# First stage of a graph kernel: products of a constant ahead of the first weights, second weights turned around the second tile's product, counts from the first tile on

## The chip, the cores and the metric

The kernel runs on one core of one Trainium2 chip. The metric is the device time of one execution in microseconds (us), as the median of several runs; lower is better. A core has TensorE (PE in the profile; its weight loads are PEld), VectorE (DVE), ScalarE (ACT), GpSimd (POOL), SyncE (SP) and 16 DMA engines. A small q behind an engine's name (SPq, POOLq) means its sequencer, which issues DMAs.

## The reference, cut to what matters

The network has four graph layers over 2708 nodes with 512 features; the adjacency matrix is 2708 x 2708, int32, zeros and ones. The change touches the first layer only:

```python
def _L0_gnn_ref(X, A, W_nb, b_nb, W_line, b_line, neibor_num):      # neibor_num = 64
    Ab = A > 0
    keep = Ab & (jnp.cumsum(Ab.astype(jnp.int32), axis=1) <= neibor_num)
    cnt = keep.sum(axis=1, keepdims=True).astype(X.dtype)
    nb_sum = keep.astype(X.dtype) @ X
    nb_mean = nb_sum / jnp.maximum(cnt, 1.0)
    xj = jax.nn.leaky_relu(nb_mean @ W_nb.T + b_nb)
    xi = jax.nn.leaky_relu(X @ W_line.T + b_line)
    return xi + jnp.where(cnt > 0, xj, jnp.zeros((), X.dtype))

x = _layernorm(x + _L0_gnn_ref(x, adj, ..., 64), axis=-1)
# then layers 1 to 3: a mean over neighbours, and two attention layers with 8 heads
```

## The kernel before, in words

Nodes are cut into 22 tiles of 128 rows (the last has 20); `rows(t)` is the height of tile t. The first stage, of some 200 us, computes three things for every tile t: `product(xT, n, wnT, ...)`, which is X times W_nb, kept as a high and a low part (`keep_y`: the high part `yH` by ACT at L241, the low part `yL` by DVE at L246); X times W_line plus its bias (`u`, added by DVE at L417, stored to `r0_dram` from POOL's queue at L418); and the masks of `HERE` = 14 of the 22 row blocks of the adjacency matrix, turned around into the resident `maskT`. The other eight masks are made in the stage behind it, while PE already multiplies masks with the kept parts.

**Weights.** `transpose_weight` (L139) fetches a 512 x 512 weight in four pieces of 128 rows into `room` (parts of `maskT` not yet in use), turns each piece with four PE transposes into a tile `ps_tr` (L146) and copies that with DVE (L147). `ps_tr` has two buffers, which the transposes of the x tiles (L134, copied by ACT at L136) use too. W_nb is turned ahead of tiles 0 and 1, W_line behind them.

**Order.** PE's order in this stage is written out by hand: `pe(ins)` (L105) ties each PE instruction behind the one before. The other queues are ordered by the framework's scheduler, which takes an instruction when by its own estimate it is ready, earlier program lines first; `tc.issue_after(ins)` holds the instructions of a block behind `ins` on its engine. The order of an engine's queue is fixed when the program is built; on the chip an engine waits for the instruction that is next in it.

**Masks.** A mask block `m` (128 x 2708 int32, cast to bf16 by the load at L282 on POOL's queue) has three buffers. Its unused last columns are cleared first: by DVE for the first two blocks, behind `weights_made`, the last copy of the turned W_line (L354); by POOL for later ones (L356). Block by block, `count` (L287, ACT, 128 x 2708) makes zeros and ones and sums them; `place` (L289) runs twice, each time on one half of the columns: a running sum (L293, DVE scan) and a product (L296, DVE). The first half is held behind the tile's `yL`, the second behind the tile's `u`. Then `turn_next` turns the block: even ones by a DMA from SP's queue (L314), with ACT taking the signs two tiles later (L319); odd ones, and those from 12 on, by 22 PE transposes (L305), with signs by ACT (L309).

**Loop.** In the main loop over t (L388) PE's order in one tile is: product with W_nb (for t > 1; tiles 0 and 1 have theirs already), the transposes of x tile t + 1, transposes of a mask if one is due, product with W_line. The sums of the W_line products lie in `pm1`, a PSUM tile with one buffer: the next such product waits until DVE has added the bias (L417). Sums of W_nb products alternate between `pm0` and a tile from `sums()`. A line decides in which tiles a block is counted:

```python
now = counted < min(HERE, -(-(t - 1) * HERE // (NT - 5)))
```

With HERE = 14 and NT = 22 this counts in tiles 2 to 6, 8 to 12 and 14 to 17; tiles 0, 1, 7 and 13 count nothing.

Of the kernel before, what the change touches and what calls it, by code (L numbers as in the profile page):

```python
# [19 lines left out]
P = 128  # L20
D = 512
KD = D // P
# [9 lines left out]
def kernel(  # L32
# [9 lines left out]
    nc = tc.nc  # L42
    N = x.shape[0]
    NT = -(-N // P)
# [6 lines left out]
    def rows(t):  # L51
        return min(P, N - t * P)
# [9 lines left out]
    ident = const.tile([P, P], F32, name="ident")  # L62
# [4 lines left out]
    ones = const.tile([P, P], F32, name="ones")  # L67
# [37 lines left out]
    def pe(ins):  # L105

        for i in ins.ins if isinstance(ins.ins, tuple) else (ins.ins,):
            if behind:
                tc.add_manual_dep(i, behind[0], mybir.DependencyInfo(
                    mybir.DependencyClass.NoSync, mybir.DependencyReason.DATA), reason="order")  # L110
            behind[:] = [i.name]
# [27 lines left out]
    def transpose_weight(room, psum, dst, src, queues=(nc.sync,)):  # L139

        for ki in range(KD):
            wr = room[ki]
            queues[ki % len(queues)].dma_start(wr, src[ki * P:(ki + 1) * P, :])
            ps = psum.tile([P, KD, P], F32, name="ps_tr")
            for ko in range(KD):
                pe(nc.tensor.transpose(ps[:, ko, :], wr[:, ko * P:(ko + 1) * P], ident))  # L146
            made = nc.vector.tensor_copy(dst[:, :, ki * P:(ki + 1) * P], ps)  # L147
        return made


    fast = ctx.enter_context(ExitStack())
# [55 lines left out]
    with ExitStack() as phase:  # L207
# [19 lines left out]
        ps_tr = phase.enter_context(tc.tile_pool(name="ps_tr", bufs=2, space=PSUM))  # L227
        ps_mm = phase.enter_context(tc.tile_pool(name="ps_mm", bufs=1, space=PSUM))
        ps_a = phase.enter_context(tc.tile_pool(name="ps_a", bufs=4, space=PSUM))
        sums = lambda dtype=F32, shape=(P, D): ps_a.tile(list(shape), dtype, name="acc", tag="acc")  # L230
# [9 lines left out]
        def keep_y(t, n, pm):  # L240
            highs[t] = nc.scalar.copy(yH(t)[:n], pm[:n])  # L241
            if t == LAST:
                low = slice(TWIN, TWIN + n)
                nc.scalar.copy(yL(t)[low], pm[low])
                return nc.vector.tensor_sub(yH(t)[low], pm[low], yL(t)[low].bitcast(F32))
            return nc.vector.tensor_sub(yL(t)[:n], pm[:n], yH(t)[:n].bitcast(F32))  # L246
# [5 lines left out]
        def product(xT, n, w, which, order=as_it_comes, pm=None):  # L252
            pm = ps_mm.tile([P, D], F32, name=f"pm{which}") if pm is None else pm
            if n == few and order is as_it_comes:
                nc.gpsimd.memset(xT[:, :, n:32], 0.0)
                for k in range(KD):
                    nc.tensor.matmul(pm[32 * k:32 * k + 32], xT[:, k, :32], w[:, k, :], start=True, stop=True)
                u = sm.tile([P, D], F32, name="u")
                nc.scalar.copy(u, pm)
                pm = sums()  # L260
                nc.tensor.matmul(pm[:TWIN + few], groups4[:, :TWIN + few], u, start=True, stop=True)
                return pm
            m = n
            if n == few:
                m = TWIN + n
                nc.gpsimd.memset(xT[:, :, n:TWIN], 0.0)
                nc.gpsimd.tensor_copy(xT[:, :, TWIN:m], xT[:, :, :n])
            for k in range(KD):
                order(nc.tensor.matmul(pm[:m], xT[:, k, :m], w[:, k, :], start=(k == 0), stop=(k == KD - 1)))  # L269
            return pm  # L270
# [4 lines left out]
        HERE = NT - 8  # L275
# [53 lines left out]
        with ExitStack() as ph:  # L329
            st = ph.enter_context(tc.tile_pool(name="l0a", bufs=1))  # L330
            wnT, wlT = weight(), weight2
            room = [maskT[:, G + k, :4 * D].bitcast(F32) for k in range(2 * KD)]

            fetches = []
            xs = early(2, NT, lambda t: fetched(x, t, rows(t), log=fetches))
            xTs = early(0, NT, lambda t, order=as_it_comes: transposed(ahead, ps_tr, xs(t), rows(t), "xT", order))

            transpose_weight(room[:KD], ps_tr, wnT, l0_w_nb, (nc.sync, nc.scalar))  # L340
            lows = {}
            for t in range(2):
                xT = xTs(t, order=pe)
                lows[t] = keep_y(t, P, product(xT, P, wnT, 0, pe))
            weights_made = transpose_weight(room[KD:], ps_tr, wlT, l0_w_line)
            b_line = bias(bcast(l0_b_line, D))
            def mask_tile():
                return st.tile([P, NT * P], BF16, name="m", bufs=3)

            def mask_rows(i):  # L350
                m = mask_tile()
                if i < 2:
                    with tc.issue_after(weights_made.ins):
                        nc.vector.memset(m[:, (0 if rows(turns[i]) < P else N - 1):], 0.0)  # L354
                else:
                    nc.gpsimd.memset(m[:, N:], 0.0)  # L356
                return load_mask(i, m)

            def by_dma(i):
                return i % 2 == 0 and i < HERE - 2  # L360

            def turned_tile():
                return end_tile(BF16)[:, :NT * P].rearrange("p (t n) -> p t n", n=P)

            masks = early(1, HERE, mask_rows)
            intos = {}

            def turn_next(i):
                if not by_dma(i):
                    for _ in turn_here(i, masks(i), lambda: sums(BF16, (P, G, P)), pe):  # L370
                        pass
                    return
                assert len(intos) < 2
                intos[i] = turned_tile()
                with tc.issue_after(fetches[-1].ins):
                    turn(i, masks(i), intos[i])
                due.append((t + 2, i))

            def signs_of(i, t):
                with tc.issue_after(highs[t].ins):  # L380
                    for _ in signs(i, intos.pop(i)):
                        pass
            masks(0)
            nc.gpsimd.memset(maskT[:, NT - 1, :], 0.0)
            nc.gpsimd.memset(maskT[:, :, N:], 0.0)
            counted = turned = 0
            due, stored = [], {}
            for t in range(NT):  # L388
                n = rows(t)
                if t == END:  # L390
                    assert not due and turned >= HERE - 2
                    ends[:] = [end_tile(F32R) for _ in range(2)]
                    for y in (yH, yL):
                        nc.gpsimd.memset(y(LAST).bitcast(F32), 0.0)
                if t > 1:

                    lows[t] = keep_y(t, n, product(xTs(t, order=pe), n, wnT, 0, pe, sums() if t % 2 else None))
                xT = xTs(t)
                if t + 1 < NT:
                    xTs(t + 1, order=pe)  # L400
                while due and due[0][0] <= t:
                    signs_of(due.pop(0)[1], t)
                while turned < min(HERE, counted - (t + 2 < NT and not by_dma(turned))):
                    turn_next(turned)
                    turned += 1
                now = counted < min(HERE, -(-(t - 1) * HERE // (NT - 5)))
                if now:
                    with tc.issue_after(stored[t - 1].ins) if t > 2 else nullcontext():
                        m = masks(counted)
                    places = st.tile([P, N // 2], BF16, name="places", bufs=1)  # L410
                    with tc.issue_after(highs[t].ins):
                        count(counted, m)
                    with tc.issue_after(lows[t].ins):
                        place(counted, m, places, 0, 2)
                pm = product(xT, n, wlT, 1, pe)
                u = sm.tile([P, D], F32, name="u")
                low = nc.vector.tensor_add(u[:n], pm[:n], b_line[:n])  # L417
                stored[t] = nc.gpsimd.dma_start(r0_dram[t * P:t * P + n, :], u[:n])  # L418
                if now:
                    with tc.issue_after(low.ins):  # L420
                        place(counted, m, places, 1, 2)
                    counted += 1
            with tc.issue_after(stored[LAST].ins):
                twins(0, turns[HERE - 1] + 1)
                twins(turns[0], NT)
# [3 lines left out]
        with ExitStack() as ph:  # L429
# [133 lines left out]
            for i, b in enumerate(cuts):  # L563
                ts_ = range(*b)
                pa = {t: sums() for t in ts_}
                for j in range(NT):
# [4 lines left out]
                    for t in ts_:  # L571
                        for y in halves(j):
                            nc.tensor.matmul(pa[t], kT[:, (t - b[0]) * P:(t - b[0] + 1) * P], y(j),  # L573
                                             start=(j == 0 and y is yH), stop=(j == LAST))
# [19 lines left out]
            for t in range(NT):  # L594
                n = rows(t)
                xT = xTs(t)
# [14 lines left out]
        with ExitStack() as ph:  # L611
            st = ph.enter_context(tc.tile_pool(name="l1b", bufs=2))
            for t in range(NT):
# [4 lines left out]
                for g0 in range(0, NT, G):  # L618
# [3 lines left out]
                    for j in range(g0, g1):  # L622
                        for y in halves(j):
                            nc.tensor.matmul(pa, mf[:, j - g0, :], y(j),  # L624
                                             start=(j == 0 and y is yH), stop=(j == LAST))
# [959 lines left out]
```

## Time and profile before

| What | us |
|---|---|
| median of 5 runs | 2904.33 |
| lowest and highest of them | 2901.45 and 2906.86 |
| the profiled execution, as timed | 2906.89 |
| its span in the profile | 2904.6 |
| PE busy in the span | 2821.3 (97%) |
| DVE busy | 1984.0 (68%) |
| ACT busy | 1501.8 (52%) |

In the profile a line of the timeline gives the start in us, the duration, the engine, the line of the kernel, the operation, output<-input with shapes, and the number of merged instructions; in square brackets stands how long the engine was idle before it, and what ended that. A line of the waits gives who waited for whom, the sum in us, how often, and the longest. A line of the windows gives one stretch of time and in it, engine by engine, busy time and number of instructions, then the granted PE clock (1.00 is full speed), the DMA engines' busy share and what they moved. PE's products in float32 show as two records each.

### The profile page before, as it was taken

The page shows a single profiled execution, that of the slowest core. Times are in us where ns is not written, and L with a number is a line of the kernel's source. Part 1 is how long each engine was busy: PE and PEld are TensorE (multiplying, and loading weights), DVE is VectorE, ACT ScalarE, POOL GpSimd, SP SyncE. Part 2 cuts the span into 40 slices and gives each one's busy share as a digit, 9 for nine tenths or more (in the row PEclk, how much of TensorE's full clock was granted, in tenths as well). Part 3 has the DMA queues.
Part 4 walks back from the last instruction along what each step waited for, and adds up shares of the span by engine and source line. Part 5 has one row for each costly group of instructions (what it writes and reads, how often), then busy time and mean ns, then how long its engine had stood idle before and what let it go on. Part 6 is the DMA issues. An engine that isn't in the chain of part 4 may idle for free. (4 is left out here: it accounts for less than half of the span.)

```text
span 2904.6 us, 35913 instructions
## 1 busy us (share of the span) xinstructions
PE 2821.3 (97%) x14062; PEld 1569.1 (54%) x14062; DVE 1984.0 (68%) x2343; ACT 1501.8 (52%) x1749; POOL 242.6 (8%) x395
## 2 busy tenths in 40 slices
PE   8999999999999999999999999999999999999998
PEld 4457765458887443444466433444385555555565
DVE  5867847443335999999978999999944435435342
ACT  3656632123223999999955999999950000000001
POOL 1111110101110000000022000000200010000011
PEclk9999999999999999999999999999999999999999
DMA  6845636322222011111153111110171000000000
GB/s 146 167 98 130 153 97 171 109 70 84 87 69 75 27 37 36 35 51 42 35 159 101 37 37 41 50 43 34 35 185 37 4 29 12 25 15 16 15 22 21
DMA packets 162005, 191.65 MB, mean 66 GB/s; under 512 B 82485, under 2 KB 107386, under 8 KB 161826
## 3 DMA queue, kind: packets, MB, share of 16 engines
q1 hardware_dynamic: 132342, 127.59, 15.7%
q0 software_dynamic: 18480, 57.45, 7.0%
q10 hardware_dynamic: 11004, 4.22, 0.6%
q8 instruction: 113, 1.85, 0.3%
q14 instruction: 66, 0.54, 0.1%
HBM read 148.91 MB, written 44.65 MB: 67 GB/s over the span
## 5 line engine op out<-in xcount | busy, mean ns | idle before, releaser
L829 DVE SCALAR_TENSOR_TENSOR e<-v_bc,ucol,maskT 128x1408 f32<-128x1408 f32 (+3 forms) x804 | 1132.1, 1468 | 321.1 <-PE pn L1212 312.3
L858 ACT ACTIVATE c<-e,bcol 128x1300 fp8e4<-128x1300 f32 (+2 forms) x688 | 956.7, 1412 | 62.2 <-DVE e L829 16.7
L1030 PE MATMUL po<-e,R 128*64 128x512 f32 (+3 forms) x4224 | 893.9, 548 | 26.4 <-DVE e L829 24.2
L1030 PEld LDWEIGHTS po<-e,R 128*64 128x64 f32 (+1 forms) x4224 | 334.1, 136 | 553.2 <-issue 389.9
L1212 PE MATMUL pn<-e,R 128*128 128x512 f32 (+3 forms) x1056 | 403.0, 545 | 1.1 <-DVE lin L1232 0.4
L1212 PEld LDWEIGHTS pn<-e,R 128*128 128x128 f32 (+1 forms) x1056 | 183.9, 190 | 197.1 <-issue 181.5
L1162 ACT ACTIVATE w<-pl,b 128x256 f32<-128x256 f32 (+1 forms) x88 | 40.9, 465 | 371.3 <-PE pl L1160 371.3
L573 PE MATMUL acc<-yH,kT 128*128 128x512 f32 x418 | 169.9, 406 | 6.7 <-ACT kT L436 4.8
L269 PE MATMUL pm<-weight,xT 128*128 128x512 f32 (+1 forms) x344 | 159.9, 608 | 9.6 <-DVE u L417 7.3
L123 POOL TENSOR_TENSOR ln_rs<-ln_rs,half 128x1 f32<-128x1 f32 (+1 forms) x88 | 55.5, 631 | 1344.1 <-DVE ln_rs L122 1337.7
L751 PE MATMUL pm<-w,xT 128*128 128x264 f32 (+1 forms) x704 | 165.1, 388 | 2.3 <-ACT xT L136 0.9
L573 PE MATMUL acc<-yL,kT 128*128 128x512 f32 x418 | 163.2, 390 | 0.0
L624 PE MATMUL acc<-yH,mf 128*128 128x512 f32 x418 | 162.7, 389 | 0.0
L624 PE MATMUL acc<-yL,mf 128*128 128x512 f32 x418 | 162.6, 389 | 0.0
L1160 PE MATMUL pl<-lin 128*128 128x256 f32 (+1 forms) x704 | 156.2, 376 | 3.4 <-DVE lin L1059 3.4
L1185 PE MATMUL pl<-lin,w 128*128 128x512 f32 x336 | 150.8, 593 | 0.0
L1160 PEld LDWEIGHTS pl<-lin 128*128 128x128 f32 x704 | 131.3, 193 | 34.7 <-issue 15.8
L751 PEld LDWEIGHTS pm<-w,xT 128*128 128x128 f32 (+1 forms) x704 | 129.6, 190 | 25.2 <-ACT xT L136 2.5
L621 ACT CAST mf<-maskT 128x1024 fp32r<-128x1024 fp8e4 (+1 forms) x66 | 64.5, 978 | 151.7 <-PE acc L624 148.1
L269 PE MATMUL pm<-w,xT 128*128 128x512 f32 x296 | 133.3, 593 | 3.2 <-ACT xT L136 2.1
L436 ACT ACTIVATE kT<-maskT 128x512 fp32r<-128x512 fp8e4 (+1 forms) x132 | 77.6, 593 | 100.6 <-PE acc L573 100.3
L930 PE MATMUL pd<-c,parts_c 128*12 128x384 fp8e4 (+2 forms) x2688 | 128.3, 307 | 0.0
(260 smaller groups left out, 2668.2 us busy)
## 6 DMA issues: line engine op xcount, KB each, us to landing
rows<-x_dram SPq DMA_DIRECT2D x63, 256.0 KB
v_bc<-v_dram SPq DMA_DIRECT2D x16, 704.0 KB
rows<-in_x_dram SPq DMA_DIRECT2D x42, 256.0 KB
x_dram<-u POOLq DMA_DIRECT2D x42, 256.0 KB, 2.4
v_bc<-v_dram SPq DMA_DIRECT2D x16, 650.0 KB
m<-in_adj_dram POOLq DMA_DIRECT2D x13, 677.0 KB, 6.9
r_dram<-u POOLq DMA_DIRECT2D x21, 256.0 KB, 3.4
rows<-r_dram SPq DMA_DIRECT2D x21, 256.0 KB
```

The lines of the kernel that those rows point to most:

```text
L269: order(nc.tensor.matmul(pm[:m], xT[:, k, :m], w[:, k, :], start=(k == 0), stop=(k == KD - 1)))
L436: made = nc.scalar.activation(kT[:, :w], maskT[:, j, b[0] * P:b[0] * P + w], AF.Relu, scale=-1.0)
L573: nc.tensor.matmul(pa[t], kT[:, (t - b[0]) * P:(t - b[0] + 1) * P], y(j), start=(j == 0 and y is yH), stop=(j == LAST))
L624: nc.tensor.matmul(pa, mf[:, j - g0, :], y(j), start=(j == 0 and y is yH), stop=(j == LAST))
L751: nc.tensor.matmul(pm[a][:m, :D // 2 + heads], xT[:, k, :m], w[:, k, a, :D // 2 + heads], start=(k == 0), stop=(k == KD - 1))
L829: self.made = nc.vector.scalar_tensor_tensor(e[:, :w], v[:, :w], ucol[:, j, h:h + 1], maskT[:, j, c0:c0 + w], op0=OP.max, op1=OP.mult)
L858: nc.scalar.activation(c[:, :w], e[:, :w], AF.Sigmoid, bias=bcol[:, j, h:h + 1], scale=STEP, saturate=False)
L930: pe(nc.tensor.matmul(p[32 * g:32 * g + 12, :c1 - c0], parts_c[:, j, h, :], c[:, c0:c1], start=(i == 0 and h == hs[0]), stop=(i == NT - 1 ...
L1030: pe(nc.tensor.matmul(po[i][HO * k:HO * k + HO, :c1 - c0], R2[at, j, h * HO:(h + 1) * HO], e[at, a:a + c1 - c0], start=(i_ == 0), stop=(i_ ...
L1160: nc.tensor.matmul(pl[:, :w], self.lin1[:, k, f * P:(f + 1) * P], h[:, k, :w], start=(k == 0), stop=(k == KD - 1))
L1185: nc.tensor.matmul(pl[:n], gT[:, f, (t - t0) * P:(t - t0) * P + n], self.lin2[:, f, :], start=(f == 0), stop=(f == KF - 1))
L1212: nc.tensor.matmul(pn[k][:, :w], R2[at, j, k * P:(k + 1) * P], e[at, :w], start=(j == 0), stop=(j == NT - 1))
```

## The change

`transpose_weight` issues its four DMAs first and then yields after each piece. Eight products of the constant `ones` (128 x 128, float32) go to PE ahead of the first weights; nothing reads their result. W_nb is turned as before. W_line's pieces 0 and 1 are turned between the transposes of x tile 1 and that tile's product with W_nb, pieces 2 and 3 behind that product; its sums lie in a tile of `sums()` instead of `pm0`. `weights_made` is now the copy of W_line's piece 0. The third mask block's last columns are cleared by DVE as well. The line that decides where blocks are counted now counts in tiles 0 to 2, 4 to 6, 8 to 10, 12 to 14, 16 and 17.

```diff
     def transpose_weight(room, psum, dst, src, queues=(nc.sync,)):
 
         for ki in range(KD):
-            wr = room[ki]
-            queues[ki % len(queues)].dma_start(wr, src[ki * P:(ki + 1) * P, :])
+            queues[ki % len(queues)].dma_start(room[ki], src[ki * P:(ki + 1) * P, :])
+        for ki in range(KD):
             ps = psum.tile([P, KD, P], F32, name="ps_tr")
             for ko in range(KD):
-                pe(nc.tensor.transpose(ps[:, ko, :], wr[:, ko * P:(ko + 1) * P], ident))
-            made = nc.vector.tensor_copy(dst[:, :, ki * P:(ki + 1) * P], ps)
-        return made
+                pe(nc.tensor.transpose(ps[:, ko, :], room[ki][:, ko * P:(ko + 1) * P], ident))
+            yield nc.vector.tensor_copy(dst[:, :, ki * P:(ki + 1) * P], ps)
...
-            transpose_weight(room[:KD], ps_tr, wnT, l0_w_nb, (nc.sync, nc.scalar))
+            warm = sums()
+            for _ in range(8):
+                pe(nc.tensor.matmul(warm[:, :P], ones, ones, start=True, stop=True))
+            first_weights = list(transpose_weight(room[:KD], ps_tr, wnT, l0_w_nb, (nc.sync, nc.scalar)))
+            line_weights = transpose_weight(room[KD:], ps_tr, wlT, l0_w_line)
             lows = {}
             for t in range(2):
                 xT = xTs(t, order=pe)
-                lows[t] = keep_y(t, P, product(xT, P, wnT, 0, pe))
-            weights_made = transpose_weight(room[KD:], ps_tr, wlT, l0_w_line)
+                if t:
+                    weights_made = [next(line_weights) for _ in range(2)][0]
+                lows[t] = keep_y(t, P, product(xT, P, wnT, 0, pe, sums() if t else None))
+            for _ in line_weights:
+                pass
...
             def mask_rows(i):
                 m = mask_tile()
-                if i < 2:
+                if i < 3:
                     with tc.issue_after(weights_made.ins):
                         nc.vector.memset(m[:, (0 if rows(turns[i]) < P else N - 1):], 0.0)
...
-                now = counted < min(HERE, -(-(t - 1) * HERE // (NT - 5)))
+                now = counted < min(HERE, -(-(t + 1) * HERE // (NT - 3)))
```

## The prediction, on record before the changed kernel was run

> **What bounds the kernel now.** I read the busy line of the page first, then PE's timeline over the start, then the windows over the first stage, then PE's and DVE's waits and one bad place in the timeline.
>
> ```profile
> PE 2821.3 (97%) x14062; PEld 1569.1 (54%) x14062; DVE 1984.0 (68%) x2343; ACT 1501.8 (52%) x1749; POOL 242.6 (8%) x395
> ```
>
> PE is the bound of the whole, so a gap that PE loses in the first stage is lost for good, and one that is closed is won, whatever the other engines do. All gaps of PE add up to 83 us; the change can reach those of the first 177 us. PE's timeline at the start:
>
> ```profile
> 4.91 3.84 PE L146 MATMUL ps_tr<-ident,maskT 128*128 128x128 f32 x16 [4.91 <-DMA maskT<-in_L_gnn_W_nb_dram]
> 8.68 1.12 PE L134 MATMUL ps_tr<-ident,rows 128*128 128x128 f32 x4
> 10.47 3.70 PE L269 MATMUL pm<-w,xT 128*128 128x512 f32 x8 [0.68 <-ACT xT L136]
> 14.01 0.60 PE L134 MATMUL ps_tr<-ident,rows 128*128 128x128 f32 x4
> 15.67 3.67 PE L269 MATMUL pm<-w,xT 128*128 128x512 f32 x8 [1.06 <-DVE yL L246]
> 19.18 1.04 PE L146 MATMUL ps_tr<-ident,maskT 128*128 128x128 f32 x8
> ...
> 23.19 5.40 PE L269 MATMUL pm<-weight,xT 128*128 128x512 f32 x8 [0.78 <-DVE weight L147]
> 28.43 0.60 PE L134 MATMUL ps_tr<-ident,rows 128*128 128x128 f32 x4
> 29.37 3.70 PE L269 MATMUL pm<-weight,xT 128*128 128x512 f32 x8 [0.34 <-DVE u L417]
> ```
>
> See here: nothing for 4.91 us; the same four transposes take 1.12 us at 8.68 and 0.60 at 14.01, so PE starts at half clock; W_line's transposes take from 19.18 to 23.19, 4.0 us, for some 1.8 of work; and the product behind them takes 5.40 instead of 3.70, 1.7 us of half clock again. The windows, cut at 36.80 and 177.00 (the W_line products of tiles 2 and 18):
>
> ```profile
> 10.50:23.20 12.70, 9.98 (x37) 5.14 (x37) 3.93 (x7) 1.66 (x3) 0.00 (x0) 1.00 0.28 83
> 23.20:36.80 13.60, 13.26 (x33) 6.08 (x34) 2.67 (x4) 0.84 (x2) 2.71 (x4) 0.87 0.54 118
> 36.80:177.00 140.20, 133.23 (x485) 65.91 (x484) 123.17 (x99) 87.33 (x115) 20.61 (x42) 0.99 0.75 149
> ```
>
> Up to 36.80 DVE is idle, then PE and DVE are both nearly full for 140 us, and PE pays for DVE:
>
> ```profile
> PE pm L269 <- DVE u L417: 7.3, 7, 2.4
> DVE places L293 <- ACT m L287: 12.6, 6, 3.8
> ```
>
> ```profile
> 108.92 2.98 DVE L293 TENSOR_TENSOR_SCAN places<-m,over 128x1354 bf16<-128x1354 bf16 x1
> 111.81 0.67 DVE L417 TENSOR_TENSOR u<-pm,bias 128x512 f32<-128x512 f32 x1
> 112.53 2.93 PE L269 MATMUL pm<-weight,xT 128*128 128x512 f32 x3 [2.43 <-DVE u L417]
> ```
>
> A bias addition queued behind a scan holds the one buffer of `pm1`. That wait of 2.43 us was followed by half clock: the product at 112.53 took 5.17 us in all, 1.5 more than 3.70. So the reach in the loop is 7.3 + 1.5 = 8.8 us.
>
> **Constant products.** `ones` is ready at 1.01 us (its memset: 0.84 + 0.17). Eight float32 products are 16 records; the nearest row is the cold transposes of the same size, 3.84 us for 16 with their gaps. So they run from about 1.05 to at most 4.9, in time in which PE has nothing. They push nothing back: the first transposes start at 4.91, on a DMA. What they can bring is full clock earlier, one measured step of 1.12 against 0.60 per four transposes. W_nb's DVE copies start at 6.03, 6.89, 7.93 and 8.79; with full clock the last two pieces and x tile 0 gain about 0.5 each, but DVE's copies (0.69 each) and two `ps_tr` buffers bind next: the first product moves from 10.47 to about 9.45. Saved 1.0, between 0 (the clock does not come) and 1.5.
>
> The trace shows that transposes alone bring the clock up: PE had nothing else from 4.91 until 10.47, and ran full there. The Trainium skill, "TensorE: Matmul & The Clock Gate", Part 4, says that transposes do not count as PE activity for the clock gate, and its Part 1 that the clock falls after an idle window of about 3.4 us. That speaks against this edit: the constants would end near 4.9, only transposes follow until 9.45, and the first product would start cold; an estimate from that page is 1.7 us more, 2900.9 in place of the 2899.2 below. I go by the rows.
>
> **Second weights.** x tile 1 is turned at 9.45 + 3.54 (10.47 to 14.01) = 13.0. Piece 0 fits into the wait that was there (1.06 us). Piece 1 needs the `ps_tr` buffer that ACT frees with x tile 1's copy, 1.3 after the transposes' start, then 0.44: the product starts at 14.7, 0.1 later than without. It no longer waits for `yL` of tile 0, having its own sums, and runs until 18.15. Pieces 2 and 3 take 0.9; DVE owes two copies of 0.69 and probably `yL` of tile 1 between them (0.68), as in the trace: the W_line product of tile 0 starts at 20.75, 2.6 after the other ended, where it was 4.0. The gap left is short of the 2.43 us at 112.53, so I take full clock: 1.7 saved, at worst 0. End of that product: 24.3 against 28.43. Sum: 1.0 - 0.1 + 1.5 + 1.7 = 4.1 us. W_line's DMAs keep their place in SP's queue (behind x rows 0 to 2), so its pieces are there as before.
>
> **Counts.** The first mask load was issued 0.46 us after the last weight copy (23.11 to 23.57). Now that copy is piece 0's, at about 15.0, so the issue is at 15.5 to 16.0. With the page's 6.9 us to landing it is there at 22.4 to 22.9, and ACT's count (2.55 + 0.19) ends at 25.1 to 25.6. POOL's queue holds nothing else then (its first store waits for `u`); the three clears on DVE (0.15, 1.23, 0.15) lie in its idle time. DMA is nearly empty until the load (0.28 in the window above).
>
> What decides is DVE's order in tile 0: the scan of block 0, ready at 25.2 or later, or tile 0's bias addition, ready at 24.3. In tile 2 of before the scan was put first (41.61, behind a wait of 3.76 for the count) and the addition at 44.50, though its product ended near 40.3. That is the nearest row, so I take scan first. Then the addition runs at 28.2 to 28.9, and tile 1's W_line product starts at 28.9 instead of 29.37; the idle 4.2 us before it cost up to 1.7 of half clock, I take 0.9. So the 4.1 us shrink to -0.4 here (from -1.2 to 0.5). With the addition first it starts at 24.95: 4.4 won.
>
> From there PE had, until 177.0, 147.6 us with the 8.8 lost. One counted tile costs DVE 2.98 + 3.03 + 2 x 0.86 + 2 x 0.67 = 9.1, another 1.3; PE's tile is 7.3 (two products of 3.43 and transposes of 0.44), plus 1.42 per block that PE turns, every second one. Before, five counted tiles of six: DVE 46.7 against PE 47.4. After, three of four: DVE 28.5 against 31.3, and DVE starts its first scan 16 us earlier (25.2, not 41.61). DVE's slack grows from 1.5% to 9%, so most waits go; some in each third counted tile stay. Lower bound of what stays 1 us, upper 8.8; I take 3.3, nearer the low end since DVE is ahead here. Won 5.5. Blocks 3 on need a turned buffer; block 0 is turned by DMA when its places end near 33, some 6 us, and load 3 then lands near 47, before tile 4 asks for it.
>
> **Sum.** -0.4 + 5.5 = 5.1 us. From 177 on PE runs the same work in the same order, its waits there (6.5 us for `kT`) hang on PE's own progress, and shift. The profiled execution took 2906.89, 2.34 more than its span and 2.56 more than the median; made against it the sum gives 2901.8, and for the median 2904.33 - 5.1 = 2899.2.
>
> **Rivals.** *Addition first in tile 0.* For it: it is ready 0.9 us before the scan. Then 4.4 is kept, and of the 8.8 about 4 stay as DVE has less lead: 4.4 + 4.8 = 9.2, 2895.1. *The waits come back from the DMA side.* The DMA engines are 0.9 busy from 60 to 120 us, and ACT waited once 2.59 us for a mask at 104.54; two more such waits that reach PE eat the 5.5: 2904, no change. Against it: masks are loaded over 18 tiles instead of 16. *Slower: the scans stand ahead of the additions in tiles 0, 1 and 2 and the masks land late.* Price: tile 0 4.2 + 1.7, tiles 1 and 2 each a scan and a product (3.0 + 0.9) and 1.5 of clock, together 16.7; less 4.1 and 4.8: 7.8 slower, 2912. It decides once these three waits pass 8.9. *The constants do nothing:* 1.0 less, 2900.2, within the first case.
>
> **How the numbers follow.** Forecast 0.47 (its own range 2895.5 to 2902.5, from the bounds above), addition first 0.28 (2892 to 2898), no change 0.15, slower 0.10. About 0.2%, 5.8 us, can be told from no change: faster means below 2898.5. That is 0.45 of the first case and nearly all of the second: 0.48; slower is the fourth, 0.10; the rest 0.42. The range 2891.5 to 2906.0 leaves out the fourth case and the ends of the others.
>
> **What would show it.** PE records of `ones` from 1.05, first product at 9.45, W_line product of tile 0 at 20.75 in 3.70 us and not 5.40; then tile 1's at 28.9 (scan first) or 24.95; waits of L269 for L417 beyond it near 3; the W_line product of tile 18 ending near 172. Wrong if tile 1's product comes after 30, or the waits sum to over 9.

## The result, and the profile after

The changed kernel takes 2910.1 us in the median (22 runs, 2903.93 to 2916.06) against 2903.35 for the kernel before in runs on the same chips (42 runs, 2900.0 to 2911.6). The ratio is 1.0019, with a 95% interval of 1.0013 to 1.0025: slower, by about 5.5 us, where 5.1 us less had been forecast. The profiled execution took 2909.59 us with a span of 2907.8. Line numbers are shifted: the product is L268 now, the count L286, the scan L292, the bias addition L423, the turning by PE L304.

The busy line of the page shows 3 us more of PE than before (2821.3), of which half clock is a part:

```profile
PE 2824.4 (97%) x14078; PEld 1571.1 (54%) x14078; DVE 1985.2 (68%) x2344; ACT 1501.5 (52%) x1749; POOL 242.3 (8%) x394
```

PE's timeline at the start of the changed kernel, cut, and two later lines of it:

```profile
1.06 3.79 PE L341 MATMUL acc<-ones 128*128 128x128 f32 x16 [1.06 <-DVE ones L68]
...
9.41 3.70 PE L268 MATMUL pm<-w,xT 128*128 128x512 f32 x8 [0.68 <-ACT xT L136]
...
14.76 3.60 PE L268 MATMUL acc<-w,xT 128*128 128x512 f32 x8
...
20.96 3.70 PE L268 MATMUL pm<-weight,xT 128*128 128x512 f32 x8 [1.72 <-DVE weight L147]
24.50 0.60 PE L134 MATMUL ps_tr<-ident,rows 128*128 128x128 f32 x4
31.22 6.38 PE L268 MATMUL pm<-weight,xT 128*128 128x512 f32 x8 [6.12 <-DVE u L423]
...
82.25 3.70 PE L268 MATMUL pm<-weight,xT 128*128 128x512 f32 x8 [1.82 <-DVE u L423]
...
107.90 5.40 PE L268 MATMUL pm<-weight,xT 128*128 128x512 f32 x8 [1.95 <-DVE u L423]
```

Up to 24.5 the start is what was forecast: first product at 9.41 (9.45), tile 1's at 14.76 (14.7), tile 0's W_line product at 20.96 (20.75) at full clock, ending at 24.5 (24.3). Then PE waits 6.12 us for tile 0's bias addition, and the product behind the wait takes 6.38 us instead of 3.70. Here are the changed kernel's ACT and DVE in that stretch, from the timeline:

```profile
22.71 1.28 ACT L286 ACT_TABLE_LOAD   x1 [3.73 <-DMA m<-in_adj_dram]
24.01 2.55 ACT L286 ACTIVATE m<-m,gate 128x2708 bf16<-128x2708 bf16 x1
26.68 2.98 DVE L292 TENSOR_TENSOR_SCAN places<-m,over 128x1354 bf16<-128x1354 bf16 x1 [5.66 <-ACT m L286]
29.70 0.87 DVE L295 TENSOR_TENSOR m<-m,places 128x1354 bf16<-128x1354 bf16 x1
30.48 0.68 DVE L423 TENSOR_TENSOR u<-pm,bias 128x512 f32<-128x512 f32 x1
```

DVE stands idle for 5.66 us in front of a scan that waits for ACT, which waits for the mask; the addition, whose product was done at 24.5, is queued behind the scan and the multiplication. The waits of PE for it, over the first stage, and the window that answers to 36.80:177.00 of before (from tile 2's W_line product to the end of tile 18's):

```profile
PE pm L268 <- DVE u L423: 12.4, 5, 6.1
```

```profile
41.30:182.20 140.90, 134.63 (x484) 66.39 (x483) 112.24 (x90) 80.91 (x110) 19.04 (x39) 0.98 0.66 138
```

DVE is less busy in it (112.24 of 140.90, where it was 123.17 of 140.20), and it is no shorter. So two things went wrong: 8.8 us at tile 1 (6.12 of waiting and 2.7 of half clock), and no relief in the loop.

### The profile page after: what moved, and what is told of

It reads as the page before. It is cut to its first block, busy times and chain, and to the rows that moved or that the text cites. A ratio compares the mean times of both kernels' runs of the same rounds, so it can differ in the third digit from the quotient of the medians.

```text
span 2907.8 us, 35944 instructions
## 1 busy us (share of the span) xinstructions
PE 2824.4 (97%) x14078; PEld 1571.1 (54%) x14078; DVE 1985.2 (68%) x2344; ACT 1501.5 (52%) x1749; POOL 242.3 (8%) x394
## 5 line engine op out<-in xcount | busy, mean ns | idle before, releaser
L268 PE MATMUL pm<-weight,xT 128*128 128x512 f32 (+1 forms) x344 | 162.5, 617 | 15.4 <-DVE u L423 12.4
L268 PE MATMUL pm<-w,xT 128*128 128x512 f32 x288 | 129.8, 593 | 2.5 <-ACT xT L136 2.1
```

## The experiments

For reading along, here is where the W_line product of a tile starts in each profile (us, from PE's timelines), and the ratio to the kernel before with its interval. Tile 21 is the last.

| Kernel | tile 1 | tile 4 | tile 21 | ratio |
|---|---|---|---|---|
| before | 29.4 | 54.1 | 197.6 | 1 |
| changed | 31.2 | 56.8 | 202.7 | 1.0019 (1.0013 to 1.0025) |
| e1 start only | 25.0 | 49.7 | 192.0 | 0.9989 (0.9980 to 0.9998) |
| e2 counts only | 27.1 | 61.5 | 213.1 | 1.0063 (1.0050 to 1.0077) |
| e3 addition first | 25.7 | 56.8 | 200.9 | 1.0015 (1.0006 to 1.0024) |
| e4 two sums | 25.1 | 57.2 | 199.4 | 1.0015 (1.0006 to 1.0024) |
| e5 start, two sums | 24.8 | 46.7 | 193.6 | 0.9994 (0.9986 to 1.0003) |
| e6 constants only | 26.6 | 51.3 | 193.7 | 0.9988 (0.9979 to 0.9996) |
| e8 weights only | 25.7 | 50.4 | 192.3 | 0.9996 (0.9987 to 1.0004) |
| e7 tile 1, held | 25.4 | 48.7 | 189.0 | 0.9985 (0.9976 to 0.9993) |
| e10 tile 1, not held | 31.8 | 58.1 | 200.1 | 1.0004 (0.9995 to 1.0013) |
| e9 start, sparser | 25.1 | 49.8 | 191.7 | 0.9986 (0.9977 to 0.9995) |

Each start is read from one execution, and half clock comes in some executions and not in others (last section). In this stage the profile of before has two stretches of it, at the products at 23.19 and 112.53, 3.2 us together; e1, e6, e7, e8 and e9 have none. So part of their lead over before in the three columns of starts is that execution's; the ratios rest on many runs.

### Which half of the change costs the time: e1 and e2

e1 is the changed kernel with the counts of before:

```diff
-                if i < 3:
+                if i < 2:
...
-                now = counted < min(HERE, -(-(t + 1) * HERE // (NT - 3)))
+                now = counted < min(HERE, -(-(t - 1) * HERE // (NT - 5)))
```

> The start of the change with the old rule for the tiles that count (2 to 6, 8 to 12, 14 to 17) and two clears on DVE. Theory (the early counts alone cost the time: the scan ahead of tile 0's bias addition took back what the start had won): W_line product of tile 0 at 21.0 as in the changed kernel, that of tile 1 at about 25.0 instead of 31.2, the loop's waits for the addition as before (near 7 us), so 4 us less than before: ratio about 0.9985. Rival (the new start itself brings nothing, since DVE, not PE, carries the loop from tile 2 on): the 4 us turn into longer waits for the addition, ratio 1.000.

Measured: 2900.35 us, ratio 0.9989, some 3 us less than before. Tile 0's product at 20.56, tile 1's at 25.04, and its waits after tile 1 are close to those of before, 7.2 us (7.0). The theory holds, though the interval leaves 1.000 out by little.

e2 is the kernel before with the two lines the other way round:

> The kernel before with the new rule for the tiles that count and three clears on DVE alone. Theory (a counted tile is tied to its own tile by its high part, so the free fourth tile does not save up slack, and the third of three counted tiles waits as the fifth of five did; the first counts come before their mask): loop waits 6 to 10 us, start 1 to 6 us later than before, ratio 1.0005 to 1.0025. Rival (three counted tiles of four relieve DVE, as predicted): waits fall to about 3, ratio 0.999 or less.

Measured: 2921.47 us, ratio 1.0063, 18 us more: worse than either theory had it. The waits of PE in e2's profile over the first stage:

```profile
PE pm L269 <- DVE u L417: 14.0, 6, 6.3
PE acc L305 <- DVE m L296: 5.6, 2, 4.0
```

The mask is loaded later there (weights made at about 23), so the first scan starts at 34.03; DVE is late up to tile 3, where PE's own order makes it wait for block 1 to be placed before it can turn it (the second line). A wait of 6.27 us at 91.34 comes on top. The theory had the kind of loss right and not its size. That the early counts, and not the start, are what costs the time is shown by the two together.

### What in the counts: e3, e4, e7, e10

e3 holds the places of block 0 behind tile 0's addition:

```diff
                     with tc.issue_after(lows[t].ins):
-                        place(counted, m, places, 0, 2)
+                        if t:
+                            place(counted, m, places, 0, 2)
...
                     with tc.issue_after(low.ins):
+                        if not t:
+                            place(counted, m, places, 0, 2)
                         place(counted, m, places, 1, 2)
```

> The changed kernel with tile 0's first half of places held behind tile 0's bias addition. Theory (the queue order on DVE in tile 0 costs 6.1 us of waiting and 2.7 of half clock): tile 1's W_line product at 25.0 instead of 31.2 and tile 2's near 34.5 instead of 41.3, of which a third comes back as later waits since DVE has less lead: 4 to 7 us less than the changed kernel, ratio to before 0.9995 to 1.0005. Rival (DVE's chain of places from 26.7 on sets the end): the same time as the changed kernel, ratio 1.002.

Measured: 2909.16 us, ratio 1.0015. Tile 1's product starts at 25.66 and tile 2's at 34.58, as the theory said, and two tiles later everything is given back. PE's timeline of e3:

```profile
43.67 0.54 PE L304 MATMUL acc<-identb,m 20*128 20x20 bf16 x12 [1.19 <-DVE m L295]
47.34 5.71 PE L268 MATMUL pm<-weight,xT 128*128 128x512 f32 x8 [3.13 <-DVE u L424]
```

In tile 3 PE waits for block 1's places, then for an addition behind the scan of block 2, then runs at half clock, and tile 4 starts at 56.8, where it starts in the changed kernel. The rival was right as far as tile 4.

e4 gives PE a second place for the W_line sums, so that it needs no addition of the tile before:

```diff
-                pm = product(xT, n, wlT, 1, pe)
+                pm = product(xT, n, wlT, 1, pe, None if t % 2 else sums())
```

> The changed kernel with the sums of every even tile's W_line product in a tile of the four-buffer pool, so that such a product does not wait for the bias addition of the tile before. Theory (the one buffer hands DVE's order on to PE): the waits for the addition (12.4 us, and 6.1 us of half clock behind them) go to under 3, 10 to 15 us less than the changed kernel, ratio to before 0.997 to 0.9985. Rival (DVE or ACT sets the pace and PE only finds another wait, for the turned x tile or a free buffer): 0 to 4 us less, ratio 1.0005 to 1.002.

Measured: 2907.58 us, ratio 1.0015, so the rival. Not one wait for the one buffer is left, and others stand in their place:

```profile
PE acc L304 <- DVE u L423: 5.9, 2, 3.3
PE acc L304 <- DVE m L295: 2.4, 1, 2.4
PE acc L268 <- ACT maskT L308: 2.1, 2, 1.2
```

The turning now waits for a buffer of the shared pool that an addition still holds, and for places; tile 4 starts at 57.2. Three ways of ordering tiles 0 to 2, and tile 4 always near 57. All three have DVE's chain of the three blocks of tiles 0 to 2, from a first scan near 27, and that chain may set it; the next two runs try that.

e7 puts that chain one tile later and keeps the addition first: counts in tiles 1 to 4, 6 to 8, 10 to 13 and 15 to 17, and block 0's scan held behind tile 0's addition.

```diff
-                now = counted < min(HERE, -(-(t + 1) * HERE // (NT - 3)))
+                now = counted < min(HERE, -(-t * HERE // (NT - 4)))
...
-                    with tc.issue_after(lows[t].ins):
+                    with tc.issue_after((low if t == 1 else lows[t]).ins):
```

> The changed kernel with the counts one tile later (tiles 1 to 4, then four of five) and the first half of block 0's places held behind tile 0's bias addition. Theory (three blocks in a row in tiles 0 to 2, from a first scan that cannot start before 26.7, make DVE late for tile 3, which waits for block 1 to be turned): tile 4's W_line product at 50 to 52, not 56.8, and the end like that of the start alone or 1 us before it: ratio 0.9985 to 0.9995. Rival (a first scan at 26.7 is late whatever follows): tile 4's product at 55 or later, ratio 1.001.

Measured: 2900.16 us, ratio 0.9985: the fastest of all by its median, though not apart from e1, e6 and e9 by the intervals. Tile 4 starts at 48.7, sooner than the theory had it. DVE in e7, and PE's waits from 29 us to the end of the stage:

```profile
24.70 0.69 DVE L423 TENSOR_TENSOR u<-pm,bias 128x512 f32<-128x512 f32 x1 [3.67 <-PE pm L268]
26.72 2.98 DVE L292 TENSOR_TENSOR_SCAN places<-m,over 128x1354 bf16<-128x1354 bf16 x1 [1.33 <-ACT m L286]
```

```profile
PE pm L268 <- DVE u L423: 4.7, 4, 1.9
```

The first scan starts at 26.72, as in the changed kernel (26.68), so a scan at 26.7 is not late in itself. Nor is the chain behind it thinner: four tiles in a row count. The third block's first scan starts at 43.72 in e3 and at 45.13 in e7. The addition behind it, in e3 and then in e7:

```profile
46.62 0.67 DVE L424 TENSOR_TENSOR u<-pm,bias 128x512 f32<-128x512 f32 x1
```

```profile
48.02 0.67 DVE L423 TENSOR_TENSOR u<-pm,bias 128x512 f32<-128x512 f32 x1
```

In e3 that addition is tile 2's and lets PE into tile 3's W_line product at 47.34; in e7 it is tile 3's and lets PE into tile 4's at 48.74. DVE is no faster in e7; PE's order asks for each block one tile later.

e10 is e7 with the hold taken out again, and nothing else.

> The changed kernel with counts from tile 1 and four of five, the scan of block 0 again ahead of tile 0's bias addition in DVE's order. Against the run with the scan held only that order differs. Theory (the order costs PE 6.1 us, and the half clock behind it up to 2.7, and with fewer blocks behind it nothing gives that back or hides it): tile 1's W_line product at 31 instead of 25.4, tile 4's at 53 to 56 instead of 48.7, ratio to before 1.000 to 1.0015. Rival (as with three blocks in a row, DVE's chain sets tile 4 either way): tile 4's product within 1.5 us of the held one's, ratio 0.9985.

Measured: 2907.68 us, ratio 1.0004. PE's line that answers to 31.22 of the changed kernel:

```profile
31.78 6.70 PE L268 MATMUL pm<-weight,xT 128*128 128x512 f32 x8 [6.44 <-DVE u L423]
```

One wait of 6.44 us with 3.0 us of half clock behind it (6.70 less 3.70), and with counts from tile 1 nothing gives it back: tile 4 is 9.4 us later than in e7, later than the theory had it. In the changed kernel the two costs lie side by side: either the order in tile 0 (e10) or counts from tile 0 on (e3) alone brings tile 4 to 57 or 58, and undoing one of them, as e3 did, hardly helps.

### Why the loop was not relieved: e9 and e5

e9 is e1 with counts a little sparser from tile 2 on: 14 blocks over 17 tiles instead of 16. By its line they fall in tiles 2 to 5, 7 to 9, 11 to 14 and 16 to 18, as ACT's counts in its trace do; the list in the expectation is not quite that.

```diff
-                now = counted < min(HERE, -(-(t - 1) * HERE // (NT - 5)))
+                now = counted < min(HERE, -(-(t - 1) * HERE // (NT - 4)))
```

> The start of the change with counts from tile 2, four tiles of five instead of five of six (tiles 2 to 5, 7 to 10, 12 to 15, 17 and 18). Against the run of the start alone only the pace differs. Theory (a sparser pace relieves the loop a little, and what the change lost lies in tiles 0 to 4): waits for the bias addition 4 to 6 us instead of 7.6, W_line product of tile 18 at 164 to 166 instead of 167.9, ratio to before 0.998 to 0.999. Rival (a sparser pace brings nothing; the run with counts from tile 1 is ahead only because it starts them earlier): waits 7 to 8 us, tile 18 at 168, ratio 0.999.

Measured: 2900.86 us, ratio 0.9986, against 0.9989 for e1: no difference that these runs can tell. The waits after tile 1:

```profile
PE pm L268 <- DVE u L423: 7.1, 6, 1.9
```

7.1 us, where e1 has 7.2. Tile 18's product starts at 165.5 against 167.9, within what the theory said, but only because one block that PE turns (1.4 us) and a wait have moved behind it: tile 21's starts at 191.7 against 192.0. The rival was right; this sparser pace by itself brings nothing, and the changed kernel's, 14 blocks over 18 tiles, kept its waits too. e7 has e9's pace and starts it one tile earlier; what it has over e9 at tile 21 (2.7 us, in one execution each) goes with that, though the times don't tell the two apart.

e5 is e1 with the second place for the W_line sums (the edit of e4).

> The start of the change with the old counts, and the sums of every even tile's W_line product in the four-buffer pool. In the run of the start alone PE waits 7.6 us for the bias addition. Theory (that order on DVE is the last thing between PE and a full loop): these waits go to under 2 and 5 to 7 us are won over the start alone, ratio to before 0.9965 to 0.997. Rival (DVE carries the loop; PE then waits for a buffer or for a block to turn, as with the new counts, where four new waits came to 12 us): 0 to 3 us won, ratio 0.998 to 0.999.

Measured: 2902.48 us, ratio 0.9994. The waits for the one buffer are gone, tile 4 starts 3.0 us sooner than in e1, and 5.9 us of waits for a buffer of the pool come back in tiles 5 and 17, the first with a half-clock stretch of 6.8 us:

```profile
PE acc L304 <- DVE u L423: 5.9, 2, 3.4
```

By the ratios e5 is 1.5 us behind e1, with intervals that overlap, so nothing was won, less than even the rival had it. Neither pace nor a buffer makes PE independent of DVE here.

### The two halves of the start: e6 and e8

e6 is the kernel before with the eight products of `ones`; e8 is e1 without them.

```diff
+            warm = sums()
+            for _ in range(8):
+                pe(nc.tensor.matmul(warm[:, :P], ones, ones, start=True, stop=True))
```

> The kernel before with the eight constant products alone. Theory (they bring full clock for W_nb's transposes, 1 us, and nothing later): first product at 9.4 to 9.9, W_line's transposes still 4 us, ratio 0.9995. Rival (they do nothing, as transposes bring up the clock by themselves): ratio 1.000, first product beyond 10.

> The kernel before with the W_line pieces turned around tile 1's product alone, no constants, old counts. Theory (it carries 3 of the 4 us that the start wins): tile 0's W_line product 2.2 to 2.6 us after the end of tile 1's W_nb product where it was 4.0, at full clock; ratio 0.999. Rival (without the constants the clock falls in the gap before tile 0's W_line product): that product takes over 5 us, ratio 0.9995 to 1.000.

Measured: 2900.94 us, ratio 0.9988 (e6), and 2902.67 us, ratio 0.9996 (e8). Their intervals overlap with each other and with e1, so these times can't say which half carries the gain. The profiles say more. In e2, which has neither half, tile 1's W_line product starts at 27.1; in e6 at 26.6, in e8 at 25.7, in e1 at 25.0. From the start of the first product to that of tile 1's W_line product it is 17.20 us in e2 and e6, with the old order of the weights, and 16.03 or 16.04 in e1, e7, e8 and e9 with the new one: the weights bring 1.2 us. What the constants bring lies ahead of that and is less certain: the first product starts at 9.01 to 9.64 in the nine profiles with them, and without them at 10.47 (before), 9.91 (e2) and 9.64 (e8). One line of e6 is worth a look, the W_line product of tile 0 behind the old order of the transposes:

```profile
22.09 3.70 PE L269 MATMUL pm<-weight,xT 128*128 128x512 f32 x8 [0.79 <-DVE weight L147]
```

It runs at full clock, as it does in e2, which has the old order too, and in e8. The 5.40 us at 23.19 in the profile of before was that execution's, not the kernel's. So e8's theory held for the start, with 2.8 us where it had 2.2 to 2.6, and its rival, a fallen clock, did not come; e6's first product, at 9.37, came as its theory had it.

## Why the prediction was wrong, point by point

Two steps failed: the price of the scan in tile 0, and the relief of the loop. Tile 2's W_line product was to start 0.4 us later than in the profile of before and started 4.5 later (41.30 against 36.78); tile 18's was to end 5.1 us earlier and ended 5.2 later (182.20 against 177.00). So 4.1 us of the miss arose up to tile 2 and 6.2 in the loop. Both signs of being wrong came: tile 1's product after 30, and waits of 12.4 us.

**The constants and the second weights** were read rightly, each start within 0.3 us. The sum of 4.1 us was too large by the 1.7 us of half clock credited to the new order of the weights: e2 and e6, with the old order, have no such half clock either. Without it the start is worth 2.4 by the prediction and 2.1 by the profiles of e1 and e2; e1's 3 us in time, 0.6 to 5.8 by its interval, are at odds with neither. Of the 2.4, the weights (1.5 less 0.1) brought 1.2. The 1.0 for the constants was counted from 10.47, the latest first product of the three profiles without them; by the means (10.0 and 9.4) it is nearer 0.6.

**Tile 0.** The order was forecast rightly, scan first, but its price was not. Forecast: addition at 28.2, tile 1's product at 28.9, half clock 0.9. Measured: addition at 30.48, product at 31.22, half clock 2.7 (6.38 less 3.70). The trace of before has this line in front of its first count, and I passed over it:

```profile
37.64 1.28 ACT L287 ACT_TABLE_LOAD   x1
```

Three parts make up the miss: ACT loads that table only when the mask has landed, so the scan starts at 26.68 and not 25.2; the multiplication (0.87) went ahead of the addition as well; and an idle stretch of 6.1 us cost 2.7 us of clock, beyond the bound of 1.7. Tile 1's product ends 4.5 us later than in the profile of before; the sum had it end 0.4 later.

**The loop.** This step failed outright. "DVE's slack grows from 1.5% to 9%, so most waits go": DVE's idle share did grow, from 12% to 20% of the window, and the waits stayed. After tile 1 the changed kernel has 6.3 us of them (12.4 less 6.1) and two half clocks of 1.7, against 7.0 and one of 1.5. e9 shows that a sparser pace alone is worth nothing that its runs can tell. What I took for a capacity is an order: an addition waits when it becomes ready while a scan is ahead of it, and a count begins only when its own tile's high part is made, so the idle time of the uncounted tile is not saved up for the next ones. In the changed kernel's trace DVE is idle behind the uncounted tile 3:

```profile
57.20 0.69 DVE L245 TENSOR_TENSOR yL<-pm,yH 128x512 fp32r<-128x512 f32 x1 [3.13 <-ACT yH L240]
60.24 2.98 DVE L292 TENSOR_TENSOR_SCAN places<-m,over 128x1354 bf16<-128x1354 bf16 x1 [2.34 <-ACT m L286]
```

Later PE's wait at 82.25, in front of tile 7's product, ends with an addition (81.52) that stood behind a scan (78.64), and the waits in front of the products of tiles 10 and 15 (1.95 and 1.94 us) end in the same way. That reading of why is from the trace; that pace does not help is from the run. The rival of the DMA side did not decide: in the loop ACT waits twice for a mask (1.69 us at 73.96, 1.41 at 142.69), while DVE works on scans of the block before, and the next scan follows without a wait for ACT.

**A cost I did not name.** Three blocks in tiles 0 to 2 load DVE with 23 us of places (three times 7.7) from 26.7 on, and PE's order asks for block 1 to be turned in tile 3. e3 shows that this alone brings tile 4 to 57; e4 gets there too, in part by a wait for a buffer of the pool into which its own edit puts sums. The slower rival had the right place and the first of its three waits; its price (16.7 us) and its second and third wait did not come.

**The rule against the constants.** The page "TensorE: Matmul & The Clock Gate" of the Trainium skill, Part 4, has it that transposes do not count for the clock gate. Here only transposes follow the constants from 4.85 to 9.41, and the product at 9.41 ran in 3.70 us, full clock; so did the first product of e8 at 9.64, with nothing but transposes ahead of it, of which the last four took 0.66 us. The row decided rightly, and the 1.7 us that the page would add did not come.

## What to carry to other kernels

Work that is moved earlier, into an engine's idle time, also moves into that engine's queue: look for what stands next in it, when its input can really be there (landing, table load and all), and who waits behind. Busy shares say little about waits of this kind; here a queue with 20% of slack kept PE waiting about as long as one with 12%, and a somewhat sparser pace or a second buffer only moved the waits. And where two limits lie side by side, undoing one of them shows less than it is worth: by the ratios e3 recovers 1 us of the changed kernel's time (no more than the intervals leave open) and e10 4, and both together (e7) 10, 0.9985 against 1.0019.

## What the runs showed of the hardware

**Half clock comes by the position of a gap, not by its length alone.** In the traces' clock records the half-clock stretches of this stage last 3.41, 6.83 or 10.24 us, one, two or three steps of a fixed grid. The windows of the changed kernel, cut by that grid, ahead of two half-clock stretches and around a gap of 1.82 us that had none:

```profile
104.85:108.27 3.42, 1.48 (x7) 0.80 (x6) 3.42 (x3) 2.72 (x3) 0.13 (x1) 1.00 0.94 173
149.22:152.63 3.41, 1.47 (x5) 0.68 (x4) 3.37 (x4) 0.89 (x2) 0.56 (x1) 1.00 1.24 199
77.54:80.96 3.42, 2.89 (x10) 1.26 (x8) 3.39 (x5) 2.54 (x5) 0.00 (x0) 1.00 0.82 157
80.96:84.37 3.41, 2.12 (x5) 1.06 (x6) 3.41 (x5) 0.14 (x1) 0.56 (x1) 1.00 1.07 200
```

And one grid step of e9, around its gap of 1.89 us in front of 133.26:

```profile
131.46:134.87 3.41, 1.61 (x4) 0.87 (x5) 3.41 (x5) 3.13 (x4) 0.56 (x1) 1.00 1.16 195
```

The second number is PE's busy time. Here grid steps in which PE was busy for 43% were followed by half clock, a step with 62% was not, nor was e9's with 47%; a gap of 1.8 to 1.9 us lies in one step or is shared by two. So e1 has a gap of 2.68 us at full clock, while 1.95 cost 1.7 us in the changed kernel, and e3 has two of 1.94 in one execution, of which one cost nothing and one 1.7:

```profile
107.83 3.70 PE L268 MATMUL pm<-weight,xT 128*128 128x512 f32 x8 [1.94 <-DVE u L424]
149.61 5.40 PE L268 MATMUL pm<-weight,xT 128*128 128x512 f32 x8 [1.94 <-DVE u L424]
```

No threshold of the busy share follows from this: a step of e3 at 41.19 with 54%, in part by products of 20 columns, was followed by half clock. The Trainium skill's page "TensorE: Matmul & The Clock Gate", Part 1, gives the free-running window of 3413 ns, which the records confirm; its rule that the clock falls after an idle window does not cover these rows, since the steps that cost the clock were 43% busy. Where a gap falls in the grid may be a part of why executions of one kernel differ by some us: of the 35 runs of the kernel before that were taken beside e5 to e8, seven with a mean granted clock of 0.998 took 2902.4 us on average, and eleven with 0.996 took 2905.9.

**A table load stands behind the wait of its activation.** ACT's load of 1.28 us at 22.71 started only when the mask had landed, after 3.73 us in which ACT was idle, so it lies on the path in full. In the trace of before the mask was there, and the load at 37.64 followed the copy ahead of it without a wait.
